# A fused transformer block: VectorE's split of q and k one step behind ScalarE's evacuation, and a projection's row statistics one and two steps behind the addition

## The chip, the cores and the metric

The kernel runs on one core of a Trainium2 chip. The time is the device time of one execution in microseconds. Three runs of the kernel before took 2398.78, 2402.26 and 2404.74 us; the median, 2402.26 us, is the time before. The execution that the hardware profiler recorded took 2406.82 us, of which 2405.1 us lie between the first and the last instruction (the span).

## The reference: what is computed

A post-norm transformer block in fp32 over x of shape (2, 2048, 256), that is 4096 rows:

```python
x = layernorm(x + attn(x))                       # 16 heads of 16, 2048 keys, no mask
x = layernorm(x + ffn(x))
# ffn(x):
n = layer_norm(x, g1, be1)
x = x + n + (n @ mix_w + mix_b)
res = x
n = layer_norm(x, g2, be2)
probs = softmax(n @ router_w)                    # 8 experts
topw, topi = top_k(probs, 2)
out = sum over the two experts e of topw * (silu(n @ w1[e] + b1[e]) @ w2[e] + b2[e])
return res + out
```

F, the width between w1 and w2, is 1024. The rotation of q and k depends on the head alone (the tables are indexed by head), and both sides of it are linear in x.

## The kernel before, in words

**Attention.** Two batches of 2048 rows, four blocks of 512 query rows each, four groups of four heads: 32 visits. A visit goes over 16 key tiles of 128 keys, so the attention loop has 512 steps. A step computes 4 score tiles of 128 keys by 512 queries (`scores`, matmuls at L470 and L479, the second of which subtracts the rows' maxima), their exponentials on ScalarE (L485), and, one step later, the products with the values (`values`, L500). The row maxima that are subtracted are computed 20 steps ahead (AHEAD) by `maxima`: four matmuls of 512 scores into ps_mx (L426) and four reductions on VectorE (L434) per step, in two halves. q and k are held in fp32 split into a high part and a remainder, stacked in DRAM (`st`) and loaded again as operands of twice or more the depth.

The order of a step is: scores and exponentials; first half of the maxima of step t + 20; `work(1.0)`; values of step t - 1; second half of the maxima. For TensorE, ScalarE, VectorE and SyncE this program order is the order on the engine (`tc.manual_schedule`); for GpSimd (POOL) a planner orders the instructions.

**What is put between.** Everything else of the block runs inside `work`: functions that `later(steps, fn, cost)` put into a heap under the step at which they are due. Those with `urgent=True` come first; `work` takes what is due until the costs of what it took reach its budget of 1.0. So a function of cost 2.0 ends the work of its step, and what is left waits for the next. In the expert part `between()` takes the place of a step: it is called after each hidden chunk and after each second matmul of the second product.

**q and k.** `prep_qk` (L338) projects 512 rows for 8 heads (matmuls L345 into ps_qk), evacuates them on ScalarE into `full` (L352), splits on VectorE (`hi` keeps the high bits, L354), subtracts on POOL (`full` becomes the remainder, L358), and writes both parts twice to the stack with four DMAs issued by POOL (L362). `full` and `hi` have two buffers each. There are 32 such calls. Ten run in the lead-in, before the loop's first step, while `leading[0]` is true; six at steps 12 to 22; and sixteen, for batch 1, between steps 41 and 177, mostly two steps apart.

**The chain of a block.** When a block of 512 query rows has been through its four groups, `block` schedules: the output projection in two halves of 256 rows (`two_products`, `project(0)` and `project(1)`), the first norms (`norms`), the mix projection in two halves (`mix`, again `two_products`), and then the second norm, the router and the lists of the experts' rows (`lists`). Blocks follow each other under `holding("chain", ...)`. `two_products` issues 8 matmuls (L561), one addition of the result to the residual on VectorE (L568), and for each of its two row groups the row statistics: `bn_stats` (L571) and `bn_aggr` (L572). After the second half, `norms` (from L611) or `lists` (from L682) is put one step later; each begins with the reciprocal root of the variances (`rsqrt`, lines 126 to 146), whose first operations are on VectorE and whose rest is on `eng`: POOL for seven blocks, VectorE for the eighth, whose chain runs in the expert part. `lists` ends with indirect DMAs on POOL that write each row to the lists of its two experts (L857).

**PSUM.** In the loop the pool of ps_mx (three banks) serves the maxima and all this work alike, ps_sc (four banks) the scores, and one bank the values.

**Expert part.** Lists of rows are worked off in tiles of 256 rows: `turn_tile` transposes the rows (ps_x, L1136) and VectorE scales them into `xT` (L1140); `hidden` computes eight chunks ps_h (L1161), each evacuated by ScalarE into hT (L1168); `add_tile` computes ps_y (L1176), which VectorE scales into `y` (L1186) and POOL adds to the output rows in DRAM by an indirect DMA (L1187). The first 21 tiles are taken from lists that do not need the eighth block, so that its chain can run among them. The final norm follows.

Of the kernel before, what the change touches and what calls it, by code (L numbers as in the profile page):

```python
# [26 lines left out]
I32 = mybir.dt.int32  # L27
AF = mybir.ActivationFunctionType
ALU = mybir.AluOpType
# [23 lines left out]
HIGH = -4096  # L53
# [10 lines left out]
def seq_postln_kernel(  # L64
# [16 lines left out]
    nc = tc.nc  # L81
# [71 lines left out]
    with ExitStack() as actx:  # L153
# [38 lines left out]
        with tc.tile_pool(name="wraw", bufs=1) as wp:  # L192
# [4 lines left out]
                out=wr.rearrange("p c h t d -> p c (h t d)"),  # L197
                in_=qkv_w.rearrange("(c p) n -> p c n", p=P),
# [4 lines left out]
                out=cs.rearrange("p a h d -> p (a h d)"), in_=rope.partition_broadcast(P)  # L203
# [4 lines left out]
            for i in range(2):  # L208
# [7 lines left out]
                out=tri,  # L216
                in_=tri,
# [31 lines left out]
            with nc.allow_non_contiguous_dma(reason="the bias, from padded heads to dense ones"):  # L249
                bias = dp.tile([P, 2, 2, 2], F32, name="bias")  # L250
                nc.sync.dma_start(out=bias.rearrange("p s hh gl -> p (s hh gl)"), in_=t3)
                for gl in range(2):
                    nc.sync.dma_start(
                        out=bqk[64 * gl : 64 * gl + 64].rearrange("p s hh -> p (s hh)"),
                        in_=bias.rearrange("(j r) s hh gl -> j r (s hh) gl", r=32)[:, 0:HD, :, gl],
# [34 lines left out]
        def later(steps, fn, cost=0.0, urgent=False):  # L290

            count[0] += 1
            heappush(todo[0 if urgent else 1], (now[0] + steps, count[0], cost, fn))
# [18 lines left out]
        leading = [True]  # L312

        def bank(name, *shape):

            if leading[0]:
                return ps_sc.tile([P, *shape], F32, name=name, tag="sc")
            return ps_mx.tile([P, *shape], F32, name=name, tag="mx")
# [19 lines left out]
        def prep_qk(b, tb, s, hh):  # L338

            full, hi = (  # L340
                ep.tile([P, 512], F32, name=k, tag=k, bufs=2) for k in ("full", "hi")
            )
            ps = bank("ps_qk", 512)
            for c in range(2):
                nc.tensor.matmul(  # L345
                    ps,
                    lhsT=wqk[:, c, s, 8 * hh : 8 * hh + 8, :].rearrange("p h d -> p (h d)"),
                    rhs=xT[b, tb][:, c, :],
                    start=(c == 0),
                    stop=(c == 1),  # L350
                )
            nc.scalar.activation(full, ps, AF.Identity, bias=bqk[:, s, hh : hh + 1])  # L352

            nc.vector.tensor_single_scalar(  # L354
                hi.bitcast(I32), full.bitcast(I32), HIGH, ALU.bitwise_and
            )
            lo = full
            nc.gpsimd.tensor_sub(lo, full, hi)  # L358
            name = f"st_{b}_{tb}_{s}_{hh}"
            t = dp.tile([8, 4, HD, 512], F32, name=name, tag=name)  # L360
            for r, part in enumerate((hi, lo, hi, lo) if s == 0 else (hi, hi, lo, lo)):
                nc.gpsimd.dma_start(out=t[:, r], in_=part)  # L362
            stack[b, tb, s, hh] = t

        def prep_v(b, kt):

# [185 lines left out]
        def small(name, *shape):  # L552
            return bp.tile([P, *shape], F32, name=name, tag=name, bufs=1)

        def two_products(name, turned_in, w, k, sum_, mv):

            ps = bank(name, 2, D)
            for i in range(2):
                at = slice((2 * k + i) * P, (2 * k + i + 1) * P)
                for c in range(2):  # L560
                    nc.tensor.matmul(  # L561
                        ps[:, i, :],
                        lhsT=turned_in[:, c, at],
                        rhs=w[:, c, :],
                        start=(c == 0),
                        stop=(c == 1),
                    )
            nc.vector.tensor_add(sum_[:, 2 * k : 2 * k + 2, :], sum_[:, 2 * k : 2 * k + 2, :], ps)  # L568
            for i in range(2 * k, 2 * k + 2):
                st = bp.tile([P, 6], F32, name="st", tag="st", bufs=3)  # L570
                nc.vector.bn_stats(st, sum_[:, i, :])  # L571
                nc.vector.bn_aggr(mv[:, i, :], st)  # L572

        xres: dict = {}

# [9 lines left out]
        def block(b, qb):  # L585
            n = b * TPB + qb


            last = n == NTB - 1
            eng, pitch, gap = (nc.vector, 1, 2) if last else (nc.gpsimd, 3, 3)  # L590
            o, xr = otok.pop((b, qb)), xres.pop(n)
            oT = bp.tile([P, 2, 512], F32, name=f"oT_{n}", tag="fT", bufs=1)
            for c in range(2):
                later(
                    c,
                    lambda c=c: turned(
                        lambda i, c: o[:, i, c * P : (c + 1) * P],
                        oT,
                        c,
                        None,  # L600
                        lambda c: rows_sb[:, ROW_BV, c : c + 1],
                        "ps_oT",
                    ),
                    0.5,
                )
            mv = small("mv1", 4, 2)

            def project(k):
                two_products("ps_p", oT, ow, k, xr, mv)
                if k == 1:  # L610
                    later(1, lambda: norms(n, xr, mv, eng, pitch, gap))  # L611

            for k in range(2):
                later(3 + 2 * pitch * k, lambda k=k: project(k), 2.0)

        def norms(n, xr, mv, eng, pitch, gap):


            z = bp.tile([P, 4, D], F32, name=f"z_{n}", tag="zx", bufs=1)
            x2 = bp.tile([P, 4, D], F32, name=f"x2_{n}", tag="x2", bufs=1)  # L620
            nT = bp.tile([P, 2, 512], F32, name=f"nT_{n}", tag="fT", bufs=1)
            mv2 = small("mv2", 4, 2)

            def normalize():

                v, r, q = (small(k, 2, 4) for k in ("v12", "r12", "q12"))
                nb = small("nb", 4)
                nc.vector.tensor_scalar_add(v[:, 0], mv[:, :, 1], EPS)
                nc.vector.tensor_scalar(
                    v[:, 1], mv[:, :, 1], 1.0 + EPS, EPS * EPS, ALU.mult, ALU.add  # L630
                )
                rsqrt(r, v, q, eng)
                r1, r2 = r[:, 0], r[:, 1]
                op_mul(eng, nb, mv[:, :, 0], -1.0, ALU.mult, r2)

                def scaled(i):
                    nc.scalar.activation(
                        z[:, i, :],
                        xr[:, i, :],
                        AF.Identity,  # L640
                        bias=nb[:, i : i + 1],
                        scale=r2[:, i : i + 1],
                    )

                def rest():
                    for i in range(4):
                        first(i)
                    nc.gpsimd.tensor_add(x2, xr, wide_rows[:, 1:2, :].to_broadcast([P, 4, D]))

                def first(i):  # L650
                    eng.tensor_scalar(
                        xr[:, i, :],
                        xr[:, i, :],
                        mv[:, i, 0:1],
                        r1[:, i : i + 1],
                        ALU.subtract,
                        ALU.mult,
                    )
                for i in range(4):
                    later(gap + (i * gap) // 3, lambda i=i: scaled(i))  # L660
                later(2 * gap, rest)
                for c in range(2):
                    later(
                        2 * gap + 2 + c,
                        lambda c=c: turned(
                            lambda i, c: z[:, i, c * P : (c + 1) * P],
                            nT,
                            c,
                            lambda c: rows_sb[:, ROW_G1, c : c + 1],
                            lambda c: rows_sb[:, ROW_BE1, c : c + 1],  # L670
                            "ps_nT",
                        ),
                        0.5,
                    )
                for k in range(2):
                    later(2 * gap + 5 + 2 * pitch * k, lambda k=k: mix(k), 2.0)

            def mix(k):

                two_products("ps_mix", nT, mixw, k, x2, mv2)  # L680
                if k == 1:
                    later(1, lambda: lists(n, xr, x2, mv2, eng, gap))  # L682

            normalize()

# [543 lines left out]
    for n, o in enumerate(os_):  # L1229
        eng = nc.gpsimd if n % 2 == 0 else nc.vector  # L1230
        mv = kp.tile([P, 4, 2], F32, name="mv", tag="mvz", bufs=4)
        for i in range(4):
# [3 lines left out]
        v, r, q, nb = (  # L1236
            kp.tile([P, 4], F32, name=k, tag=k, bufs=4) for k in ("vz", "rz", "qz", "nbz")
        )
# [92 lines left out]
```

## Time and profile before

| quantity | value |
|---|---|
| median of the runs (lowest, highest) | 2402.26 us (2398.78, 2404.74) |
| profiled execution | 2406.82 us |
| its span | 2405.1 us |
| mean granted TensorE clock | 0.972 of full |
| TensorE busy | 2277.9 us (95%) |
| VectorE busy | 1534.9 us (64%) |
| ScalarE busy | 1374.4 us (57%) |
| GpSimd busy | 512.7 us (21%) |
| attention loop, 300 to 600 us: TensorE / VectorE / ScalarE busy | 293.65 / 237.98 / 204.23 us |
| start of the expert part, 1800 to 1900 us: TensorE busy, clock | 84.04 us, 0.88 |
| expert part, 1900 to 2100 us: TensorE busy, clock | 200.00 us, 1.00 |

How to read the rows: engines are PE (TensorE matmuls), PEld (its weight loads), DVE (VectorE), ACT (ScalarE), POOL (GpSimd) and SP (SyncE); L12 is line 12 of the kernel. A row of the timeline has the start in us, the busy us, the engine, line and operation, the result and what it is made from, the shapes, and how many instructions were taken together. In square brackets is the idle time before it and what ended that, as inferred from semaphores. A row of the waits has the engine, what waited and its line, what it waited for, the total in us, how many times, and the longest. The page's group rows have busy us and mean ns of one after the first bar, and the idle time before them after the second. PEclk is the granted clock as a share of full speed.

### The profile page before, as it was taken

To read this page: it belongs to the slowest core of one execution; us is meant where nothing else is said; L and a number is where in the kernel's file an instruction comes from. 1 tells how busy PE (TensorE), PEld (TensorE's weight loads), DVE (VectorE), ACT (ScalarE), POOL (GpSimd) and SP (SyncE) were. 2 spreads that over 40 slices of the span, in tenths; PEclk is the share of its full clock that TensorE was granted. 3 is DMA by queue.
4 is the path that set the end of the run, shared out by engine and by line. 5 is a ranking of instruction groups with operands and counts; after the bars stand their busy time and mean duration, and the time that the engine had idled before them with its cause. 6 is when DMAs were issued, how large, how long until landed. Compare 5 with 4: busy or idle time off the path is not lost.

```text
span 2405.1 us, 39739 instructions
## 1 busy us (share of the span) xinstructions
PE 2277.9 (95%) x14270; PEld 1363.8 (57%) x14270; DVE 1534.9 (64%) x3060; ACT 1374.4 (57%) x2722; POOL 512.7 (21%) x863
## 2 busy tenths in 40 slices
PE   5899999999999999999999999999998899999993
PEld 2444555545545555555555555555547788888883
DVE  2678778868877887888888888888825111111113
ACT  1167667757766776777777667777773222223333
POOL 6212221140123022011211202202122322222113
PEclk7799999999999999999999999999999899999997
DMA  7516541141124211111311211221045466567994
GB/s 217 153 42 182 144 115 54 54 132 53 53 72 123 87 55 58 58 45 54 115 45 54 71 45 53 89 71 53 1 138 168 142 193 180 176 182 225 291 292 151
DMA packets 175516, 269.69 MB, mean 112 GB/s; under 512 B 29776, under 2 KB 109656, under 8 KB 175320
## 3 DMA queue, kind: packets, MB, share of 16 engines
q1 hardware_dynamic: 142648, 213.26, 25.9%
q0 software_dynamic: 32256, 52.98, 10.1%
q8 instruction: 113, 1.85, 0.3%
q10 hardware_dynamic: 416, 0.92, 0.1%
q14 instruction: 83, 0.68, 0.1%
HBM read 204.29 MB, written 62.74 MB: 111 GB/s over the span
## 4 chain that ended last, share of the span: by engine, by line
PE 77%; DVE 16%; DMA 3%; ACT 2%; issue 1%; POOL 1%; another core or an unknown queue 0%; SPq 0%; ACTq 0%; DVEq 0%; POOLq 0%
PE av L500 19%; PE ps_mx L426 13%; DVE pm L434 12%; PE ps_h L1161 11%; PE ps_y L1176 10%; PE ps_sc L470 6%; PE ps_sc L479 6%; PE ps_qk L345 2%; DMA st<-full 2%; PE ps_v L371 1%; PE ps_p L561 1%; PE ps_mix L561 1%; PE ps_m L458 1%; PE ps_o L522 1%; PE ps_b L766 1%
## 5 line engine op out<-in xcount | busy, mean ns | idle before, releaser
L434 DVE TENSOR_REDUCE pm<-ps_mx 128x1 f32<-128x512 f32 x2048 | 1273.2, 682 | 218.3 <-PE ps_mx L426 209.3
L485 ACT ACTIVATE ex<-ps_sc 128x512 f32<-128x512 f32 x2048 | 1058.1, 603 | 453.7 <-PE ps_sc L479 433.7
L426 PE MATMUL ps_mx<-km,qm 64*128 64x512 f32 x2048 | 580.5, 474 | 36.4 <-DMA km<-st 15.3
L426 PEld LDWEIGHTS ps_mx<-km,qm 64*128 64x128 f32 x2048 | 297.7, 186 | 556.2 <-DVE pm L434 357.4
L500 PE MATMUL av<-ex,vt 128*32 128x512 f32 x4096 | 547.3, 606 | 0.0
L470 PE MATMUL ps_sc<-qm,km 64*128 64x512 f32 x2048 | 435.4, 396 | 0.4 <-ACT ex L485 0.3
L479 PE MATMUL ps_sc<-mrow,sel 64*128 64x512 f32 x2048 | 428.6, 392 | 0.0
L1168 ACT ACTIVATE hT<-ps_h,b 128x256 f32<-128x256 f32 (+1 forms) x368 | 156.3, 425 | 378.3 <-PE ps_h L1161 361.9
L1161 PE MATMUL ps_h<-xT,w 128*128 128x256 f32 (+1 forms) x1472 | 282.6, 342 | 17.2 <-issue 11.0
L1161 PEld LDWEIGHTS ps_h<-xT,w 128*128 128x128 f32 x1472 | 231.6, 193 | 62.4 <-ACT hT L1168 21.7
L1176 PE MATMUL ps_y<-w,hT 128*128 128x256 f32 x1136 | 253.7, 379 | 0.0
L479 PEld LDWEIGHTS ps_sc<-mrow,sel 64*128 64x128 f32 x2048 | 216.7, 185 | 40.5
L470 PEld LDWEIGHTS ps_sc<-qm,km 64*128 64x128 f32 x2048 | 214.8, 186 | 42.0 <-ACT ex L485 18.3
L1176 PEld LDWEIGHTS ps_y<-w,hT 128*128 128x128 f32 x1136 | 212.1, 190 | 27.5 <-issue 0.7
L1140 DVE TENSOR_SCALAR xT<-ps_x,cols_sb 128x256 f32<-128x256 f32 (+1 forms) x92 | 40.2, 478 | 271.4 <-PE ps_x L1136 271.4
L1187 POOL DMA_INDIRECT acc<-y,xg x71 | 110.1, 1551 | 390.8 <-DVE y L1186 307.0
L500 PEld LDWEIGHTS av<-ex,vt 128*32 128x32 f32 x4096 | 80.9, 108 | 133.7 <-issue 132.6
L1186 DVE TENSOR_SCALAR y<-ps_y,xg 128x256 f32<-128x256 f32 x71 | 34.2, 483 | 187.8 <-PE ps_y L1176 187.6
L132 POOL TENSOR_SCALAR op_mul<-mv 128x4 f32<-128x4 f32 x18 | 4.2, 233 | 492.7 <-DVE mv L572 491.7
L358 POOL TENSOR_TENSOR full<-full,hi 128x512 f32<-128x512 f32 x32 | 40.9, 1279 | 239.5 <-DVE hi L354 239.4
L345 PE MATMUL ps_qk<-xT,wqk 128*128 128x512 f32 x128 | 73.3, 700 | 4.8 <-ACT xT L336 1.5
L857 POOL DMA_INDIRECT x_list<-zx,at_i x64 | 64.1, 1002 | 16.5 <-issue 13.6
(198 smaller groups left out, 1160.4 us busy)
## 6 DMA issues: line engine op xcount, KB each, us to landing
w<-in_w SPq DMA_DIRECT2D x92, 1024.0 KB
km<-st SPq DMA_DIRECT2D x256, 256.0 KB
st<-hi POOLq DMA_DIRECT2D x64, 256.0 KB
st<-full POOLq DMA_DIRECT2D x64, 256.0 KB
qm<-st SPq DMA_DIRECT2D x64, 256.0 KB
xg<-x_list SPq DMA_DIRECT2D x25, 258.0 KB
x_in<-in_x SPq DMA_DIRECT2D x8, 512.0 KB
xr<-in_x SPq DMA_DIRECT2D x8, 512.0 KB
```

The costliest lines, as they stand in the source:

```text
L345: nc.tensor.matmul(ps, lhsT=wqk[:, c, s, 8 * hh : 8 * hh + 8, :].rearrange("p h d -> p (h d)"), rhs=xT[b, tb][:, c, :], start=(c == 0), st ...
L426: nc.tensor.matmul(ps[j], lhsT=qm[w][pair][r, qt * P : (qt + 1) * P], rhs=km[w][pair][r, kb * 512 : (kb + 1) * 512], start=True, stop=True,)
L434: nc.vector.tensor_reduce(pm[w][:, qt, 2 * pair + j, kb : kb + 1], ps[j], AX.X, ALU.max)
L470: nc.tensor.matmul(sc[j], lhsT=km[w][pair][r, kt * P : (kt + 1) * P], rhs=qm[w][pair][r, :], start=True, stop=False,)
L479: nc.tensor.matmul(sc[j], lhsT=sel[pair][r, :], rhs=mrow[w][r, :], start=False, stop=True)
L485: nc.scalar.activation(ex, sc[j], AF.Exp, scale=0.25)
L500: nc.tensor.matmul(av[32 * h : 32 * h + 32, :], lhsT=vt[b][:, kt, at : at + 32], rhs=exs[h], start=(kt == 0), stop=(kt == 15),)
L857: ins = nc.gpsimd.indirect_dma_start(out=x_list, out_offset=bass.IndirectOffsetOnAxis(ap=at_i[:, k, i : i + 1], axis=0), in_=zx[:, k, i, : ...
L1161: nc.tensor.matmul(ps, lhsT=w1t[:, c, k * P : (k + 1) * P], rhs=xT[:, c, :], start=(c == 0), stop=(c == 1),)
L1168: nc.scalar.activation(hT[:, k, :], ps, AF.Silu, bias=b1[:, k : k + 1])
L1176: nc.tensor.matmul(ps, lhsT=hT[:, k, s * P : (s + 1) * P], rhs=w2t[:, k, :], start=(k == 0), stop=(k == NFC - 1),)
L1187: nc.gpsimd.indirect_dma_start(out=acc, out_offset=bass.IndirectOffsetOnAxis(ap=xg[:, s, D : D + 1].bitcast(I32), axis=0), in_=y, in_offse ...
```

## The change

Three edits, with no instruction added or removed:

- In `prep_qk`, the split (`hi`), the subtraction and the four DMAs of the stack are put into a function, which runs at once in the lead-in and otherwise is due one step later. There it runs in that step's `work`, behind the first half of the maxima.
- In `two_products`, the statistics of the two row groups are no longer issued directly behind the addition; the first is due one step later, the second two steps later.
- `norms` and `lists`, which need the statistics, are put three steps behind the second half rather than one.

```diff
@@ prep_qk
             nc.scalar.activation(full, ps, AF.Identity, bias=bqk[:, s, hh : hh + 1])
-
-            nc.vector.tensor_single_scalar(
-                hi.bitcast(I32), full.bitcast(I32), HIGH, ALU.bitwise_and
-            )
-            lo = full
-            nc.gpsimd.tensor_sub(lo, full, hi)
             name = f"st_{b}_{tb}_{s}_{hh}"
             t = dp.tile([8, 4, HD, 512], F32, name=name, tag=name)
-            for r, part in enumerate((hi, lo, hi, lo) if s == 0 else (hi, hi, lo, lo)):
-                nc.gpsimd.dma_start(out=t[:, r], in_=part)
             stack[b, tb, s, hh] = t
+
+            def split():
+
+                nc.vector.tensor_single_scalar(
+                    hi.bitcast(I32), full.bitcast(I32), HIGH, ALU.bitwise_and
+                )
+                lo = full
+                nc.gpsimd.tensor_sub(lo, full, hi)
+                for r, part in enumerate((hi, lo, hi, lo) if s == 0 else (hi, hi, lo, lo)):
+                    nc.gpsimd.dma_start(out=t[:, r], in_=part)
+
+            if leading[0]:
+                split()
+            else:
+                later(1, split)
@@ two_products
             nc.vector.tensor_add(sum_[:, 2 * k : 2 * k + 2, :], sum_[:, 2 * k : 2 * k + 2, :], ps)
-            for i in range(2 * k, 2 * k + 2):
+
+            def moments(i):
                 st = bp.tile([P, 6], F32, name="st", tag="st", bufs=3)
                 nc.vector.bn_stats(st, sum_[:, i, :])
                 nc.vector.bn_aggr(mv[:, i, :], st)
+
+            for i in range(2):
+                later(1 + i, lambda i=i: moments(2 * k + i))
@@ block, project(k)
                 if k == 1:
-                    later(1, lambda: norms(n, xr, mv, eng, pitch, gap))
+                    later(3, lambda: norms(n, xr, mv, eng, pitch, gap))
@@ norms, mix(k)
                 if k == 1:
-                    later(1, lambda: lists(n, xr, x2, mv2, eng, gap))
+                    later(3, lambda: lists(n, xr, x2, mv2, eng, gap))
```

## The prediction

> **What bounds the kernel now.** The page's first part and its chain of work come first.
>
> ```profile
> PE 2277.9 (95%) x14270; PEld 1363.8 (57%) x14270; DVE 1534.9 (64%) x3060; ACT 1374.4 (57%) x2722; POOL 512.7 (21%) x863
> ...
> PE 77%; DVE 16%; DMA 3%; ACT 2%; issue 1%; POOL 1%; another core or an unknown queue 0%; SPq 0%; ACTq 0%; DVEq 0%; POOLq 0%
> ...
> L434 DVE TENSOR_REDUCE pm<-ps_mx 128x1 f32<-128x512 f32 x2048 | 1273.2, 682 | 218.3 <-PE ps_mx L426 209.3
> ```
>
> TensorE is the bound on average, but the chain runs through VectorE for 16%, in the attention loop. The timeline of a plain attention step shows why:
>
> ```profile
> 229.11 2.48 DVE L434 TENSOR_REDUCE pm<-ps_mx 128x1 f32<-128x512 f32 x4 [0.21 <-PE ps_mx L426]
> 231.80 2.48 DVE L434 TENSOR_REDUCE pm<-ps_mx 128x1 f32<-128x512 f32 x4 [0.21 <-PE ps_mx L426]
> ```
>
> Steps follow each other every 2.70 us. VectorE is busy 2.48 and waits 0.21; TensorE has no slack either, since its next maximum matmul needs the bank that a reduction frees. Reductions start every 0.60 us (the four starts within 2.48), and the last-to-first distance is 0.89, so an extra VectorE operation finds about 0.30 us of cover in a plain step and delays TensorE one for one beyond it. Where a step carries other TensorE work, VectorE's extra work lies beside that. The timeline around a q/k projection:
>
> ```profile
> 257.19 1.98 PE L345 MATMUL ps_qk<-xT,wqk 128*128 128x512 f32 x4
> ...
> 259.98 0.43 DVE L354 TENSOR_SCALAR hi<-full 128x512 int32<-128x512 int32 x1 [1.65 <-ACT full L352]
> 260.63 2.48 DVE L434 TENSOR_REDUCE pm<-ps_mx 128x1 f32<-128x512 f32 x4 [0.23 <-PE ps_mx L426]
> 263.33 2.48 DVE L434 TENSOR_REDUCE pm<-ps_mx 128x1 f32<-128x512 f32 x4 [0.23 <-PE ps_mx L426]
> ```
>
> VectorE waits 1.65 us for the evacuation at L352, but TensorE is in the 1.98 us projection meanwhile, and the reduction after the split (260.63) again ends its wait on TensorE. The next step is a plain 2.70. So the wait that the change takes away costs nothing today. A projection of a block, by the TensorE starts of its first score matmul in successive steps:
>
> ```profile
> 1701.08 0.43 DVE L571 BATCH_NORM_STATS2 st<-x 128x6 f32<-128x256 f32 x1
> 1701.54 0.18 DVE L572 BATCH_NORM_AGGREGATE mv<-st 128x2 f32<-128x6 f32 x1
> 1701.58 0.40 PE L470 MATMUL ps_sc<-qm,km 64*128 64x512 f32 x2
> ...
> 1704.63 0.39 PE L470 MATMUL ps_sc<-qm,km 64*128 64x512 f32 x2
> ```
>
> The step after the addition is 1704.63 - 1701.58 = 3.05 instead of 2.70: the two statistics pairs do cost 0.36 us here. The last place is the start of the expert part:
>
> ```profile
> 1815.98 8.24 PE L1161 MATMUL ps_h<-xT,w 128*128 128x256 f32 x24 [3.88 <-issue]
> ...
> 1815.35 0.99 DVE L1140 TENSOR_SCALAR xT<-ps_x,cols_sb 128x256 f32<-128x256 f32 x2
> ```
>
> and, in the windows (busy time of PE, PEld, DVE, ACT, POOL, then PEclk),
>
> ```profile
> 1800.00:1900.00 100.00, 84.04 (x376) 68.23 (x376) 38.46 (x161) 31.24 (x59) 32.48 (x29) 0.88 0.51 162
> ```
>
> The timeline's first row calls the wait issue, but xT is late: VectorE works off the last block's statistics and its reciprocal root from 1811.56 to 1815.43 before xT. The window's PEclk is 0.88.
>
> **The change, part by part.** Nothing is added or removed. All sums are against the profiled execution's 2406.82 us (span 2405.1), 4.56 above the median 2402.26.
>
> *Splits.* Ten of the 32 q/k calls run in the lead-in and stay. 22 move; their `hi` now runs in the next step, after its first two reductions. (a) In five of the 22 the next step has TensorE work (row maxima turned, ps_o, ps_n2T or another projection): hidden. In about ten it is plain: `hi` has 0.43 us, of which the following instruction starts 0.34 later, against a cover of 0.30: 0.05 each, +0.5; without cover 0.34 each, +3.4. (b) In six it joins other small VectorE work (after the maxima's last reduction, or the choice of experts) that has used the cover: six by 0.34 less what the longer step hides, taken +0.7 (bounds 0 and +2.0). In the last the split comes after a step whose budget is spent, and is one more step late: in (c).
>
> (c) POOL's subtraction and its four stack DMAs move with it. `full` and `hi` have two buffers, so the evacuation two calls on, on ScalarE ahead of the exps, waits for these DMAs. Today that wait shows in the lead-in only:
>
> ```profile
> ACT full L352 <- DMA st<-full: 46.7, 8, 7.3
> ```
>
> In the loop, `full` two calls on comes 14.2 to 15.2 us after `hi`; the last DMA packet lands 9.0 to 12.9 us after it, and the lead-in rows put some 1.2 between landing and the evacuation. With `hi` 2.9 us later the distance becomes about 12. ScalarE may be about 1.3 late before TensorE is. At most pairs 9.2 + 1.2 still fits; in the two places where the split is two steps late and key loads run beside it (landing 12.5) I take 1.4 us each, and once 0.85 in batch 0: +3.7. Here the Trainium skill has a rule: "DMA: Bandwidth & Descriptors", section on the SWDGE path, gives a DMA issued by GpSimd about 2.0 us plus its bytes at 436 GB/s. By it (an estimate) subtraction 1.29, four issues of 0.6 and 2.6 for the last are 6.3 us: no evacuation would wait, and (c) would be 0. The trace shows 9.0 to 12.9, and decides: +3.7 (bounds 0 and +12, the latter if all eleven second calls lose 1.1). Splits together: +4.9.
>
> *Statistics in the loop.* A pair (0.43 + 0.18, following instruction 0.55 later) in a plain step costs 0.55 - 0.30 = 0.25. Before, two pairs after an addition cost 0.36, once (where root operations follow in the same stretch) 0.59. After, two pairs in two plain steps cost up to 0.50, or 0.25 where one of them lies under the next block of TensorE work (turned maxima, a second projection); the root's four operations that follow keep their own step (2.94 against 2.70, so 0.24, as before). For a block's four additions: 0.36 to 0.50 for the two first halves, 0.59 to 0.25 + 0.24 for the second halves, so +0.28 - 0.20, about +0.1; with the 0.04 that a trace of steps resolves, I take 0 for seven blocks (+0.6 at most). Without cover, 28 additions bring two pairs of 0.55 instead of 0.25: 56 x 0.30 = +16.8; with all hidden, 28 x -0.36 = -10.
>
> *Block chains.* Norms and lists come two steps later each, so the lists are some 10 us late. Seven blocks have slack: the first tile's gather starts at 1771.67 and attention ends at 1797.3, so 10 us lie under attention; if that cover were gone they would be paid. The bias addition of a next block's residual now stands ahead of POOL's root chain of 14 operations (4.0 us); it leaves the normalizing evacuation at most 0.4 us late, under TensorE work: 0. SP's queue gets the block's store behind the next loads, which no one waits for: 0.
>
> *Start of the expert part.* The eighth block runs between tiles. Now `xT` of tile 1 stands ahead of the last pair and of the root chain. VectorE: addition 1810.84 to 1811.5, pair 0.55, then xT as soon as ps_x ends (1812.1) and the queue is free, about 1812.7; TensorE resumes near 1813.3, 1.2 us idle instead of 3.88: -2.7. What the clock does decides the rest. In this trace the matmul distance doubles (0.216 to 0.427 us) between 1814.88 and 1821.71, 5.73 us of it in work, so about 2.9 us lost. The Trainium skill's "TensorE: Matmul & The Clock Gate", part 1 on the clock gate, has an idle window of some 3.4 us halve the clock; a wait of 1.2 would not. By the rule -2.9 more, by the trace alone (no wait of that length at that place) 0 to -2.9; I take the rule, as the row's 3.88 did halve it. Sum -5.6 (bounds -2.7, -5.6).
>
> *Tile 3.* Its eight ps_h stall beside the block's 16 indirect stores:
>
> ```profile
> 1866.89 2.07 PE L1161 MATMUL ps_h<-xT,w 128*128 128x256 f32 x4 [1.74 <-issue]
> 1872.56 2.08 PE L1161 MATMUL ps_h<-xT,w 128*128 128x256 f32 x4 [3.60 <-issue]
> 1878.22 5.28 PE L1161 MATMUL ps_h<-xT,w 128*128 128x256 f32 x12 [3.58 <-ACT hT L1168]
> ```
>
> With 1.77 before them, 10.7 us, and half clock again after. I don't know the cause of these slow hand-overs. The stores now come about 6 us later against the tiles (four steps of about 1.7): taken -3, bounds -12 and +4.
>
> Sum: +4.9 + 0 - 5.6 - 3 = -3.7; since tile 3's share is the least sure I leave 1.4 of the gain out: -2.3. The profiled run would take 2404.5; from the median, 2402.26 - 2.3 = **2400.0**.
>
> **Rivals.** *Stack writes become the wait (slower).* Place: `full` at L352 behind the stores of two calls earlier, on ScalarE ahead of the exps. It decides where landing plus 1.2 passes about 13.5 us after `hi`. For it: 12.9 is seen already, and 46.7 us of this wait stand in the lead-in. Against: most landings are near 9.3. Where it landed last in the lead-in (11.3 to 14.4 us), landing at 14.1 gives 14.1 + 1.2 - 12.2 - 1.3 = 1.8 for each of eleven calls, 19.8 instead of the 3.7 in the sum: -2.3 + 16.1 = +13.8, so 2416. It is slower than the bound below from 1.2 a call, landing at 13.5.
>
> *Both stalls of the expert part go (faster).* If tile 3's 10.7 us and the second half-clock stretch (17.07 us long) go, -12 to -18 in all: 2388. For it: one 16-store burst is beside all four waits. Against: the burst still meets some tile.
>
> *Nothing happens.* The wait at the split (VectorE on L352: 77.4 us in 31 waits) was hidden, the pairs cost alike, and the tile start moves its wait to the next late thing: about 2402. It belongs with the forecast.
>
> **Chances.** Measurement can tell about 0.3%, 7.2 us: below 2395.1 is faster, above 2409.5 slower. Forecast with "nothing", 0.41, own range 2395 to 2409; faster rival 0.27; slower rival 0.32. To leave out no more than 2 in 10, the range goes from the faster rival's 2388 to 2420, a little past the slower one's 2416: about 1 in 10 is left out on each side.
>
> **What would show it.** Right: no wait of VectorE on L352 in the loop and q/k steps unchanged near 4.8; steps with a pair at about 2.95; ps_h of tile 1 within 1.5 us of ps_x and PEclk above 0.9 in 1800 to 1900. Wrong: "full <- DMA st<-full" well over 46.7 us; plain steps with a pair at 3.25; the 3.88 wait back before another row.

## The result

The changed kernel takes 2399.3 us, the kernel before in the same series 2403.73 us. The ratio is 0.9978, with a 95% interval of 0.9968 to 0.9988: 5.3 us faster by the ratio, within the 0.3% called no change, against a forecast of 2.3 us. The profiled execution took 2394.76 us (span 2393.0), 12.1 less than the one profiled before, so the two traces lie further apart than the two kernels. The total came out close; two of its terms, the chains of the blocks and the splits, did not.

The page of the changed kernel, in the rows that answer to those shown before (busy time, chain by engine, the reductions; its lines are up to 11 higher than before):

```profile
PE 2268.4 (95%) x14270; PEld 1358.4 (57%) x14270; DVE 1531.5 (64%) x3060; ACT 1374.4 (57%) x2722; POOL 511.4 (21%) x863
...
PE 71%; DVE 21%; DMA 3%; issue 2%; POOL 1%; ACT 1%; SPq 1%; ACTq 0%; POOLq 0%; DVEq 0%
...
L441 DVE TENSOR_REDUCE pm<-ps_mx 128x1 f32<-128x512 f32 x2048 | 1272.1, 682 | 267.7 <-PE ps_mx L433 260.9
```

The same work, but VectorE has 21% of the chain instead of 16%. The waits (engine, what waits, for what: total us, times, longest):

```profile
ACT full L352 <- DMA st<-full: 51.6, 10, 8.7
DVE hi L359 <- ACT full L352: 36.8, 9, 9.9
```

VectorE's wait for the evacuation fell from 77.4 us to 36.8 in 9, all of them in the lead-in: in the loop it is gone, as the change intends. What that was worth shows in the timeline around the q/k projection shown before:

```profile
255.16 0.69 ACT L352 ACTIVATE full<-ps_qk,bqk 128x512 f32<-128x512 f32 x1 [0.83 <-POOL xr L592]
...
256.54 2.48 DVE L441 TENSOR_REDUCE pm<-ps_mx 128x1 f32<-128x512 f32 x4 [2.31 <-PE ps_mx L433]
...
258.94 0.42 DVE L359 TENSOR_SCALAR hi<-full 128x512 int32<-128x512 int32 x1
259.27 2.47 DVE L441 TENSOR_REDUCE pm<-ps_mx 128x1 f32<-128x512 f32 x4
```

The reductions after the projection now wait 2.31 us for TensorE in one piece, where 1.65 for ScalarE, the split and 0.23 stood: nothing gained. The split lies among the reductions a step later, in a step of 2.70.

The start of the expert part is the place that gained. The timeline of ps_h and the window (PE, PEld, DVE, ACT, POOL, PEclk):

```profile
1813.76 5.42 PE L1172 MATMUL ps_h<-xT,w 128*128 128x256 f32 x24 [1.04 <-ACT hT L1179]
...
1860.05 1.13 PE L1172 MATMUL ps_h<-xT,w 128*128 128x256 f32 x4 [0.29 <-issue]
1863.59 1.13 PE L1172 MATMUL ps_h<-xT,w 128*128 128x256 f32 x4 [2.42 <-issue]
1869.34 2.08 PE L1172 MATMUL ps_h<-xT,w 128*128 128x256 f32 x4 [4.61 <-issue]
```

```profile
1800.00:1900.00 100.00, 89.74 (x430) 74.37 (x431) 39.00 (x164) 33.93 (x66) 33.87 (x30) 0.97 0.55 176
```

TensorE resumes after 1.04 us instead of 3.88 and at full clock (24 matmuls in 5.42 us, before 8.24). Tile 3 waits 0.29 + 2.42 + 4.61 = 7.3 us instead of 10.7.

Three lengths are used below. The *lead-in* ends at the first exponential of step 0; the *loop* goes from there to the first exponential of step 511; the *start* goes from ps_x of tile 0 to ps_x of tile 6. Before: 125.1, 1669.0 and 113.9 us. After: 120.8, 1673.9 and 102.0. The lead-in is not touched by the change and lies between 120 and 126 in the variants (114 in the one that gives it a buffer more), so 4 us of the difference between the two traces mean nothing. The loop became 4.9 longer, the start 12 shorter. Single executions also have one to four stretches of half clock in the loop, nearly all of 3.41 us, costing about 1.5 each (a step of 3.72 took 5.28).

### The profile page after: what moved, and what is told of

It reads as the page before. It is cut to its first block, busy times and chain, and to the rows that moved or that the text cites. A ratio compares the mean times of both kernels' runs of the same rounds, so it can differ in the third digit from the quotient of the medians.

```text
span 2393.0 us, 39741 instructions
## 1 busy us (share of the span) xinstructions
PE 2268.4 (95%) x14270; PEld 1358.4 (57%) x14270; DVE 1531.5 (64%) x3060; ACT 1374.4 (57%) x2722; POOL 511.4 (21%) x863
## 4 chain that ended last, share of the span: by engine, by line
PE 71%; DVE 21%; DMA 3%; issue 2%; POOL 1%; ACT 1%; SPq 1%; ACTq 0%; POOLq 0%; DVEq 0%
PE av L507 17%; DVE pm L441 17%; PE ps_mx L433 13%; PE ps_h L1172 11%; PE ps_y L1187 10%; PE ps_sc L477 5%; PE ps_sc L486 5%; PE ps_qk L345 2%; DMA st<-full 2%; PE ps_v L378 1%; PE ps_p L568 1%; PE ps_mix L568 1%; PE ps_m L465 1%; PE ps_x L1147 1%; PE ps_o L529 1%
## 5 line engine op out<-in xcount | busy, mean ns | idle before, releaser
L1172 PE MATMUL ps_h<-xT,w 128*128 128x256 f32 (+1 forms) x1472 | 276.8, 338 | 12.3 <-issue 7.3
L352 ACT ACTIVATE full<-ps_qk,bqk 128x512 f32<-128x512 f32 x32 | 22.0, 687 | 80.4 <-DMA st<-full 51.6
```

The lines of the kernel that those rows point to most:

```text
L1172: nc.tensor.matmul(ps, lhsT=w1t[:, c, k * P : (k + 1) * P], rhs=xT[:, c, :], start=(c == 0), stop=(c == 1),)
```

## The experiments

**What made the loop longer.** There are two theories. S is the prediction's sum: the splits cost 4.9 us, the statistics nothing. P is a collision, and came from comparing each VectorE instruction's duration in the two traces. One row stands out, the first operation of `lists`, 128x4 numbers, 0.16 us in the loop before. The changed kernel's timeline:

```profile
1305.11 2.45 DVE L441 TENSOR_REDUCE pm<-ps_mx 128x1 f32<-128x512 f32 x4
...
1306.60 2.40 POOL L592 TENSOR_TENSOR xr<-xr,wide_rows 128x1024 f32<-128x1024 f32 x1 [6.16 <-DMA xr<-in_x]
...
1307.48 1.55 DVE L704 TENSOR_SCALAR v<-mv 128x4 f32<-128x4 f32 x1
...
1309.06 0.17 DVE L137 TENSOR_SCALAR q<-v 128x4 int32<-128x4 int32 x1
```

It takes 1.55 us and ends at 1309.02, 0.03 after GpSimd's addition of the bias to the next block's residual (ends 1308.99). The reductions, which read PSUM, run at 0.68 beside that same addition. Six of the seven blocks in the loop have it: 0.43, 1.16, 0.63, 0.37, 1.39 and 1.36 us too long, 5.3 in all, and the six steps take 3.32 to 4.33 where 2.95 is normal: 5.3 again. `lists` is four steps later than it was, and so meets an addition whose time is set by its DMA. The Trainium skill, "SBUF — State Buffer", section "Who interferes with whom", has it: VectorE's tensor-scalar forms can use a second port that they share with GpSimd; whoever is first keeps it for the whole instruction and the other stands still, while a tensor reduction never contends. The holds agree with that; no run here shows the port itself.

The trace of the kernel before has one such hold already, in the expert part, where `lists` of the eighth block meets another addition of GpSimd:

```profile
1834.19 2.35 POOL L708 TENSOR_TENSOR xr<-xr,x 128x1024 f32<-128x1024 f32 x1 [7.60 <-DVE x L568]
...
1835.28 1.28 DVE L693 TENSOR_SCALAR v<-mv 128x4 f32<-128x4 f32 x1
```

1.28 us for the operation that takes 0.16 elsewhere, ending 0.02 after the addition: the cost could be read before the change.

In the edits below, what stands in brackets or dots is shortened. *split_only*: the kernel before with the first edit alone.

```diff
-            (split, subtraction and four DMAs at once)
+            if leading[0]: split()
+            else: later(1, split)
```

> The kernel before with the split's edit alone. Loop = first exponential of step 0 to that of step 511: 1669.0 us before, 1673.9 after (+4.9). Theory P (shared port: the +4.9 is the variance operation of lists, held while GpSimd adds the next block's bias to the residual): no such collision here, so the loop is only the one evacuation that waits for the stack (step 18, about +1.3) and some tenths longer, +0.5 to +2; start of the expert part as before (TensorE resumes 3.9 after ps_x of tile 1). Total +0.5 to +2, ratio 1.000 to 1.001. Theory S (the prediction's sum: the splits cost 4.9 and the statistics nothing): loop +4 to +6, ratio 1.0015 to 1.0025.

Measured: ratio 1.0012 (0.9999 to 1.0024), 2.9 us slower; loop 1673.5, with one stretch of half clock more than before; no held operation. The ratio falls between the two theories. Step by step, seven steps that carried other small VectorE work take 0.32 to 0.35 more, together 2.4; plain steps take nothing more; the wait for the stack cost 0.1. So the splits alone do lose time in these steps, half of S's 4.9; the ratio alone does not tell them from nothing. The timeline of one of the seven:

```profile
270.35 0.19 DVE L461 TENSOR_TENSOR mt<-nm,mt 128x16 f32<-128x16 f32 x1
270.45 1.28 DVE L442 TENSOR_REDUCE pm<-ps_mx 128x1 f32<-128x512 f32 x2
271.65 0.41 DVE L360 TENSOR_SCALAR hi<-full 128x512 int32<-128x512 int32 x1
271.98 2.48 DVE L442 TENSOR_REDUCE pm<-ps_mx 128x1 f32<-128x512 f32 x4
```

The last maxima operation and the split are 1.3 us apart with no idle time between: the cover is spent once, the split pays its whole 0.33.

*stats_only*: the other two edits alone.

```diff
-            for i in range(2 * k, 2 * k + 2):  (statistics at once)
+                later(1 + i, lambda i=i: moments(2 * k + i))
-                    later(1, lambda: norms(...));  later(1, lambda: lists(...))
+                    later(3, lambda: norms(...));  later(3, lambda: lists(...))
```

> The kernel before with the statistics' edits alone (moments one and two steps behind, norms and lists three steps behind). Theory P: the variance operation of lists takes 0.5 to 1.6 us instead of 0.16 in six blocks, the loop is 4 to 5 us longer; start of the expert part 8 to 13 us shorter as in the changed kernel; total -4 to -8, ratio 0.997 to 0.9985. Theory S: loop unchanged, total -8 to -13, ratio 0.9945 to 0.9965.

Measured: ratio 0.9965 (0.9956 to 0.9975), 8.4 us faster; six held operations of 0.78 to 1.82 us; loop 1674.3, with three stretches of half clock more than before; start 99.7. The held operations are P's; the ratio is at the edge of S's range and decides nothing.

*lists_later*: the changed kernel with one number changed.

```diff
-                    later(3, lambda: lists(n, xr, x2, mv2, eng, gap))
+                    later(3 if n == NTB - 1 else 4, lambda: lists(n, xr, x2, mv2, eng, gap))
```

> The changed kernel with lists four steps behind the second half instead of three (the eighth block stays at three), so that its first VectorE operation falls behind GpSimd's residual addition. Theory P: no variance operation over 0.3 us in the loop, step of the root's first operations 2.93 instead of 3.0 to 4.3, loop about 5 us shorter than in the changed kernel, total about -10 against before, ratio 0.995 to 0.997. Theory S: nothing but the step moves, ratio as the changed kernel, 0.9978.

Measured: ratio 0.9950 (0.9931 to 0.9968), loop 1670.0, 3.9 shorter than in the changed kernel. The same place in its timeline:

```profile
1307.63 2.38 POOL L592 TENSOR_TENSOR xr<-xr,wide_rows 128x1024 f32<-128x1024 f32 x1 [7.08 <-DMA xr<-in_x]
...
1310.33 0.16 DVE L704 TENSOR_SCALAR v<-mv 128x4 f32<-128x4 f32 x1
```

The operation starts 0.3 us behind the addition and takes 0.16; none in the loop is held. At the six places the held step and the next one together take 5.3 us less than in the changed kernel: S is out, and the +5.3 belongs to the collision. The loop as a whole is only 3.9 shorter, because in this execution the evacuation of step 177 waits 6.12 us for the stack; TensorE stands 2.14 us behind it, half clock follows, and the step takes 8.77 where the changed kernel's takes 6.42.

*residual_pieces*: the changed kernel with GpSimd's addition in four.

```diff
-            nc.gpsimd.tensor_add(xres[n], xres[n], (row, broadcast to 4))
+            for i in range(4):
+                nc.gpsimd.tensor_add(xres[n][:, i], xres[n][:, i], wide_rows[:, 0, :])
```

> The changed kernel with GpSimd's addition to the residual as four instructions of 256 numbers per partition instead of one of 1024 (2.4 us). Theory P (VectorE's variance operation is held for as long as one GpSimd instruction has the port): the held operation waits for at most one piece, so it takes 0.16 to 0.8 us instead of 0.5 to 1.8, the loop is 3 to 4 us shorter than in the changed kernel, ratio 0.9955 to 0.997. If it is held by anything else (its operand, a semaphore, GpSimd's queue as a whole), its durations stay at 0.5 to 1.8 and the ratio at 0.9978.

Measured: ratio 0.9980 (0.9969 to 0.9991): the durations went as P said, the total did not. The loop is 1679.8, with one stretch of half clock of 10.24 us and two of 3.41. Its timeline:

```profile
1517.43 2.80 POOL L593 TENSOR_TENSOR xr<-xr,wide_rows 128x256 f32<-128x256 f32 x4 [6.20 <-DMA xr<-in_x]
...
1518.28 0.61 DVE L705 TENSOR_SCALAR v<-mv 128x4 f32<-128x4 f32 x1
...
1518.92 0.65 DVE L137 TENSOR_SCALAR q<-v 128x4 int32<-128x4 int32 x1
1519.61 0.65 DVE L140 TENSOR_SCALAR r<-q 128x4 int32<-128x4 int32 x1
```

Each VectorE operation gets in behind one piece, and the next one is held by the next piece. Over the six blocks the holds on v, q and r sum to 5.7 us, as much as one long hold. So a hold ends with each GpSimd instruction and begins again with the next, and shorter GpSimd instructions do not help a row of such VectorE operations.

**What made the expert part shorter.** *last_only* applies the statistics' edits to the eighth block alone, *all_but_last* is the changed kernel with the eighth block as before.

```diff
# last_only, c = (n == NTB - 1); all_but_last, c = (n < NTB - 1)
+                if c: later(1 + i, ...moments...)   else: moments(2 * k + i)
+                    later(3 if c else 1, lambda: norms(...))
+                    later(3 if c else 1, lambda: lists(...))
```

> The kernel before with the statistics' edits for the eighth block alone (the one whose chain runs among the expert tiles); split and seven blocks as before. Both theories: loop unchanged (1669), TensorE resumes about 1.0 to 1.2 us after ps_x of tile 1 and keeps the full clock there; total -8 to -13, ratio 0.9945 to 0.997. If the gain of the expert part in the changed kernel's trace (12.7 us) was mostly that execution's luck at tile 3, -4 to -6, ratio 0.9975 to 0.9985.

> The changed kernel with the eighth block's statistics, norms and lists as before. Loop as in the changed kernel (+4 to +6 against before); TensorE resumes 3.9 us after ps_x of tile 1 again, with half clock after it; total +4 to +6, ratio 1.0015 to 1.0025. If the eighth block is not what makes the changed kernel faster, ratio 0.998.

Measured: last_only 0.9948 (0.9930 to 0.9966), 12.5 us faster than before, loop 1671.4 with two stretches of half clock more, start 102.4; all_but_last 1.0025 (1.0013 to 1.0036), 6.0 us slower, loop 1675.0, start 112.2, TensorE resuming after 3.87. So the eighth block makes the whole gain, and the rest of the change is a loss of some 6 us.

*more_stores* asks what makes the hand-overs at tile 3 slow.

```diff
+            for e in range(E):
+                nc.gpsimd.indirect_dma_start(out=spare, ..., in_=none)
```

> The changed kernel with eight more indirect stores on GpSimd behind the eighth block's sixteen, into a tensor that nothing reads (work added, about 10 us of GpSimd's queue). If the slow hand-overs to ScalarE at tile 3 come from the burst of indirect stores, they go on for about 10 us longer: idle TensorE between tiles 0 and 6 at 15 to 25 us instead of 11, ratio 1.000 to 1.005. If not, idle stays at 8 to 11 us and the ratio at 0.998.

Measured: ratio 0.9992 (0.9980 to 1.0005), idle TensorE 11.4 us. The added stores were spread from 1877.5 to 1913.9 among the tiles' own, and the tile was in its second product, which needs no hand-over to ScalarE, when most of them ran, so the times decide nothing. The traces say a little more. In the nine others of the chips that have the slow hand-overs, the last of them ends 24.2 to 24.6 us after the first of the sixteen stores is issued, whether it is the fifth chunk of the tile or the eighth; with eight stores more it ends at 28.5. So the end goes with the stores and not with the tile. This is one trace, and it does not say what holds the hand-overs up.

**A version from both.** *stats_lists4* is stats_only with lists four steps behind (the edit of lists_later): no split moved, no hold.

> The version that the runs point to: the split as before, statistics one and two steps behind the addition, norms three and lists four steps behind (three for the eighth block). From the four runs before: seven blocks -0.4 each = -3 in the loop, no held variance operation, none of the splits' +3; start of the expert part -12 as in the run with the eighth block alone. Total -13 to -16, ratio 0.9935 to 0.9945, at least as fast as the eighth block alone (0.9948).

Measured: 2391.64 us, ratio 0.9949 (0.9937 to 0.9961), loop 1666.1. A smaller gain than expected, and level with last_only and lists_later. What the later statistics and chains do in the loop is read from periods of 64 steps, one block each, without a half-clock stretch (us from first exponential to first exponential; two or three values are different kernels):

| kernels | steps 264 to 328 | 328 to 392 | 392 to 456 |
|---|---|---|---|
| before, split_only, last_only | 204.5, 204.6, 204.6 | 205.4, 204.7, 204.7 | 204.5, 205.4 |
| changed | 204.5 | 205.5 | 205.4 |
| lists_later | 203.8 | 203.8 | 203.8 |
| stats_lists4 | 203.7 | 203.6 | 203.7 |

About 0.8 us less per block where `lists` is four steps behind; the changed kernel's rows have the holds in them. The prediction took 0. Where the gain lies shows when a block's steps are cut in two and each part's excess over plain steps of 2.70 is summed (periods from step 256 on). The first part, up to two steps before the transposes ps_n2T, has the projection, the norms and the mix with all pairs and roots: 18.6 to 18.7 us per block before, 18.6 in the changed kernel with the hold left out, 18.6 in stats_lists4. The moved pairs cost and gain nothing. The second part has the router and the choice of experts: 13.0 to 13.2 before (13.9 in one period of three), 12.7 in the changed kernel, 12.3 in stats_lists4; on the two chips of the next runs, 12.7 before and 12.3 after. So what gains, 0.4 per block (0.7 in stats_lists4), is the choice of experts at its later place: in stats_lists4 it lies in the step of the transposes ps_o. This holds for the blocks whose chains run in steps 200 to 456. The seventh gains 1.5 (0.6 on the other chips), at the loop's end; in the first two the q and k projections run alongside, and no gain can be told.

**The buffers and the spread.** *three_buffers* gives `full` a third buffer; before_again, after_again and best_again repeat three kernels. These ran on two other chips, called the quiet ones below, because tile 3 has no slow hand-overs there; the others are the first chips.

```diff
-ep.tile([P, 512], F32, name=k, tag=k, bufs=2)
+ep.tile([P, 512], F32, name=k, tag=k, bufs=3 if k == "full" else 2)
```

> The changed kernel with three buffers for `full` instead of two (`hi` keeps two). In the changed kernel one evacuation in the loop waits 2.7 us for the stack's DMAs (step 18, 6.10 us long instead of 4.79), two more wait 0.6 and 1.4 without a longer step. If `full` is what is waited for, all three waits go and step 18 takes 4.8 to 4.9; if it is `hi` (still two buffers), VectorE waits there instead and step 18 or 19 stays 1 us or more longer. The variance operations stay held (0.5 to 1.8 us), so the loop is 1 to 1.5 us shorter than in the changed kernel's trace (1673.9), apart from stretches of half clock (3.4 us each, up to 1.7 us of time).

> The kernel before once more, for the spread between executions. Expected: lead-in 120 to 126 us (125.1 in its first trace, 120 to 125 in those of the variants), loop 1668 to 1671 us with one to three stretches of half clock, TensorE resuming 3.9 us after ps_x of tile 1 with half clock after it, idle TensorE between tiles 0 and 6 at 15 to 17 us.

Measured: three_buffers 2374.51 us, before_again 2382.81, one run each. With the third buffer ScalarE's waits for the stack fall from 51.6 us in 10 (changed kernel) to 8.2 in 2, and the lead-in from 120.8 to 114.1: it was `full` that was waited for. The evacuation of step 18, first in the changed kernel, then with three buffers:

```profile
184.47 0.69 ACT L352 ACTIVATE full<-ps_qk,bqk 128x512 f32<-128x512 f32 x1 [3.45 <-DMA st<-full]
```

```profile
176.03 0.69 ACT L352 ACTIVATE full<-ps_qk,bqk 128x512 f32<-128x512 f32 x1 [0.83 <-issue]
```

Step 18 takes 6.10 us in the changed kernel and 4.79 here: that wait cost 1.3. It differs from execution to execution: the other kernels with the split moved and two buffers have 4.79 to 6.20 there. Two later waits (1.2 and 0.5 us longer in the changed kernel) lie in steps with other TensorE work and did not lengthen them; in lists_later the last one did.

In before_again tile 3 is quiet. Its ps_h of tiles 1 and 3, and those of after_again:

```profile
1808.00 7.11 PE L1161 MATMUL ps_h<-xT,w 128*128 128x256 f32 x24 [3.87 <-issue]
...
1852.81 7.18 PE L1161 MATMUL ps_h<-xT,w 128*128 128x256 f32 x32
```

```profile
1808.52 5.42 PE L1172 MATMUL ps_h<-xT,w 128*128 128x256 f32 x24 [1.04 <-ACT hT L1179]
...
1851.66 5.45 PE L1172 MATMUL ps_h<-xT,w 128*128 128x256 f32 x24
```

Thirty-two matmuls in a row without a wait: the slow hand-overs of tile 3 are absent on these two chips and present in every trace of the others. The early wait and its cure are in both. The loop of before_again, 1664.9, is also 4.1 below that of the first trace of the same kernel, so loops are compared on the same chips only.

> The changed kernel once more. In the trace of the kernel before that was taken last, the hand-overs to ScalarE at tile 3 were not slow (tile 3 took 18.9 us instead of 33.3) and five burst steps of the loop were 1.0 to 1.4 us shorter; in all that execution was 24 us shorter. If that came with the chip, then on such a chip the changed kernel gains only at the start of the expert part (-6) and loses in the loop (+5 to +7): ratio 0.999 to 1.001; on a chip with slow hand-overs 0.997 to 0.9985 as first measured. Tile 3 takes 20 us in the first case and 25 to 31 in the second.

> The version with the split as before and lists four steps behind, once more beside the changed kernel. Without slow hand-overs: start -6, loop -3, so -9 or ratio 0.996; with them -12, ratio 0.994 to 0.996. In both cases 5 to 9 us faster than the changed kernel.

Measured: after_again 0.9994 (0.9984 to 1.0004), start 92.2 against before_again's 98.4, loop 1668.8 against 1664.9, held operations 5.2 us in all. best_again 2375.08 us, 0.9949 (0.9932 to 0.9967), loop 1663.9, start 92.2. The version is as good on both kinds of chip; the change itself is worth 0.2% on one and nothing that can be told on the other.

## Why the prediction was right in total and wrong in two steps

| step | predicted, us | measured, us | from |
|---|---|---|---|
| split in plain steps | +0.5 | 0.0 | steps of split_only |
| split beside other small work | +0.7 (0 to 2.0) | +2.4 | seven steps, split_only |
| evacuations that wait for the stack | +3.7 (0 to 12) | +1.3 (0.1 in split_only, 3.2 in lists_later) | step 18, three_buffers |
| statistics in the loop | 0 (-10 to +17) | 0 | first part of the blocks |
| block chains: what GpSimd holds | 0 | +5.3 | six held operations |
| block chains: the choice of experts | 0 (not priced) | about -3 (-2 on the quiet chips) | four blocks by 0.4, one by 1.5 (0.6) |
| tile 1 and its clock | -5.6 | -5.5; -4.3 on the quiet chips | wait and 24 matmuls, 3.88 and 8.24 against 1.04 + 0.19 and 5.42 |
| tile 3 and the rest of the start | -3 (-12 to +4) | about -6; -2 on the quiet chips | what is left of the starts: 113.0 (mean of 3) to 101.9 (mean of 6); 98.4 to 92.2 |

The start as a whole gained 11.1 us on the first chips and 6.2 on the quiet ones. With it the measured terms sum to 2.4 + 1.3 + 0 + 5.3 - 3 - 11.1 = -5 on the first chips, against the measured -5.3 (2.4 either way), and, with the 0.4 that step 18 lost there, to 2.4 + 0.4 + 5.2 - 2 - 6.2 = -0.2 on the quiet ones, against -1.4 (2.4 either way).

**The step that failed** is *Block chains*: "the bias addition of a next block's residual now stands ahead of POOL's root chain ...: 0". It saw which GpSimd instruction the moved chain meets, priced the queue, and did not ask what VectorE's first operation shares with it. Had it done so, from nothing to 2.4 us in each of six blocks was the bound, and 5.3 is inside it; the 1.28 us in its own trace showed the size. That the step did not spoil the total is luck. The same step missed a gain, the choice of experts at its new place, of about 3 us, and the sum took the splits 1.2 too dear and the gain of the start 2.5 too small. The gain is read from steps and was not tried alone.

*Statistics in the loop*: right. A pair in a plain step costs 0 (first behind a step with other TensorE work) to 0.23, and over a block the moved pairs come to nothing, as the sum had it.

*Splits*: the mechanism "hidden in TensorE's longer step today, so nothing gained" held. The mis-sized terms are the joined steps (seven at the full 0.34, not six less a discount, and past the bound of 2.0) and the buffer waits, of which one and not three reached TensorE in this trace; a wait of 2.6 us more than usual cost 1.3, which agrees with the 1.3 of slack that the sum used. Of the two values for the stack's DMAs the trace's was right: at step 18 `full` came 14.7 us after the `hi` two calls earlier and was still waiting, where the rule's estimate of 6.3 would have left no wait.

*Start of the expert part*: resumption was put at 1.2 us and came at 1.04; at this place the rule on the clock gate was right to be taken. All four traces with the wait of 3.87 or 3.88 have half clock behind it, 6.8 us in the first and 3.4 in the other three, so the clock's share is 2.8 or 1.7 us; none of the ten with 1.04 (1.03 in one) has. A new wait of 1.19 at tile 2 gives a little of it back: ScalarE's evacuation now stands behind the scaling of the rows (zx), which waits for VectorE's root chain, and in that chain the first operation is again held by a GpSimd addition, for 0.7. On the quiet chips 1.7 of the 6.2 is another half-clock stretch, at tile 2 of before_again; nothing shows that the change took it away.

*Rivals*: the slower one (stack writes) did not come in the changed kernel: it needed eleven waits of 1.2. It is not far off, as step 177 of lists_later shows (6.12 us of wait). The faster one is not reached by the change, -5.3, but the version without its losses reaches -12. Tile 3 stayed partly: 7.3 of 10.7 us here.

## What to carry to other kernels

When a chain is moved by some steps, look for what it meets on engines that do not seem to take part: here one VectorE operation of 0.16 us waited out a GpSimd instruction of 2.4, and moving the chain one step further gave 5 us back at the six places. The trace before had one example of it; a tiny instruction that takes eight times its usual time is worth asking about. A delay that helps one block can cost in the others; the gain was in the last block, where VectorE's chain stood ahead of what TensorE waited for, and applying it there alone was worth more than applying it everywhere. And cover is spent once per step: two small operations in one step pay the second in full.

## What the runs showed of the hardware

- VectorE's one-input operations on SBUF (a scalar addition on 128x4 numbers, a shift and a multiply-add on int32) stand still until the end of a GpSimd addition that is already running, to within 0.03 us, one GpSimd instruction at a time; reductions from PSUM do not (0.68 us beside it).
- Hand-overs from TensorE to ScalarE of 1 to 11.5 us (from the end of a chunk's matmuls to the start of its evacuation), between 7 and 25 us after the first of the eighth block's list stores, on some chips and not on others, with the same program. With them tile 3 takes 25 to 33 us, without 19 to 20. Their cause is open.
- Half clock comes in stretches of 3.41 us and multiples. In the loop it appears one to four times in an execution and costs about 1.5 us for each 3.41; two traces of one kernel can differ by 3 us in the loop for that alone. Of the 33 in the loops of the fourteen traces, 23 begin within 4.5 us behind the start of one of the router's 16 matmuls of 8 columns each (ps_l), which run seven times in a loop, and in all 23 TensorE had been idle for no more than 0.11 us at a time in the 6.8 us before. So a long wait is not the only thing that half clock follows here.
